# A 26-product scheme of 256-unit blocks in five of the seven outer terms of a graph network's adjacency products

## The chip, the cores and the metric

The kernel runs on one core of one Trainium2 chip. The metric is the device time of one execution in microseconds; the median of a few runs counts. The engines of the core are PE (matrix products; PEld is its weight load), DVE, ACT and POOL (elementwise work) and SP, which here only issues transfers. Each engine works through its own queue in order.

## The reference

Four layers on x, 8 batches x 2048 nodes x 64 features, with one 2048 x 2048 adjacency matrix A, all in float32. Each layer ends with `x = layernorm(x + layer(x))`.

```python
# layer 0: a weight matrix of its own for each node
w = einsum('nd,dkio->nkio', embedding, weight);  b = einsum('nd,do->no', embedding, bias)
As = [eye, A, 2 * (A @ A) - eye]
out0 = einsum('bnki,nkio->bno', einsum('knm,bmc->bnkc', stack(As), x), w) + b
# layer 1: twice  z = relu((A z) w_i)
# layer 2: x w_self + (A x) w_neigh + bias
# layer 3: [x, A x, 2 A A x - x, the last two again] w + bias
```

With the products by A regrouped this takes seven products of A with a 2048 x 512 matrix (512 = batch x feature): 1 and 2 in layer 0, 3 and 4 in layer 1, 5 in layer 2, 6 and 7 in layer 3.

## The kernel before

**Products 2 to 7** are calls of `product`. It cuts A into 2 x 2 blocks of 1024 and the right side into 2 x 2 quarters of 1024 x 256, and forms seven outer terms instead of eight (A11, S1, A12, S2, S4, S3, A22, in this order; S1 to S4 are sums of blocks of A). The sums of the right side are the tiles `T` (t1 to t4, DVE). Each outer term calls `inner`, which does the same once more with blocks of 512 and quarters of 512 x 128: four sums `t` on DVE (L258), and seven products `mul`, each of four matmuls with 512 moving columns (L286). In products 5 and 7 (`onto_slot`) the output stands the other way round, and a `mul` is sixteen matmuls with 128 moving columns (L279). `inner` works with three PSUM banks (mma, mmb, mmc); DVE and ACT add the results into tiles `C` (u, v, c), lines L229, L304, L332. From there `feature` functions are queued in a `Pump`, which puts a step of them behind each `mul`.

The blocks of A and of its sums come from memory in chunks of 1 MB, `load(q, s)`, seven to a term, through a ring of four buffers (seven after `to_late`), issued by SP. The sums of blocks (`comb`) are made in product 1 by `prepare` on DVE, and stored from POOL's queue by `keep`; of the four raw blocks of S1 to S4 `put` stores three.

**Layer 0's per-node product** (`feature0`) follows product 2's terms: 64 tiles of 128 nodes x 2 batches, four to a job. For each tile PE makes y in two halves (L1154; PSUM tiles `y`, three buffers). DVE multiplies the first half by the embedding and sums it into xy (eight times L1164); ACT does the second half (eight times L1168) into `s`, which POOL adds up in three halvings (L1173) and adds to xy (L1175). `s` has two buffers. The inputs xT and tT of a job are fetched on SP's queue when the job before it begins. `pump.run(n)` lets whole jobs run between terms: four jobs behind S2, four behind S3, and the other eight, 32 tiles, in product 3 behind its term A11.

The order on each engine is made at build time by a scheduler that goes by readiness and its own cost estimates; `keep_in_program_order` pins single instructions. What stands in one engine's queue is executed in that order, whatever comes earlier at run time.

`to_late` (called by product 3 through `between`) closes the pools of layer 0 and opens `p_mm2`, `p_z` and `ring2`. Before, product 3 called it behind S1.

Of the kernel before, what the change touches and what calls it, by code (L numbers as in the profile page):

```python
# [16 lines left out]
P = 128  # L17
# [4 lines left out]

A11, A12, A22, S1, S2, S3, S4 = range(7)
A21 = 7

DONE = (0, 3, 2, 1)


class Pump:


    def __init__(self):
        self.jobs = []
        self.later = []
        self.rate = 1
        self.gate = None
        self.owed = 0
        self.hold = False  # L40

    def add(self, gen):
        self.jobs.append(gen)
# [28 lines left out]
                if next(job[2], "done") == "done":  # L72
                    self.later.remove(job)

    def run(self, n=None):

        while self.jobs and n != 0:
            for _ in self.jobs[0]:
                self.tick()
            self.jobs.pop(0)  # L80
            n = None if n is None else n - 1

    def step(self, n=1, now=False):
        if self.jobs and self.hold and not now:
# [20 lines left out]
def kernel(  # L105
# [26 lines left out]
    NP = B // 2  # L132
    DH = D // 2
    RING = 4
    BLK = TG * GW

    big = ctx.enter_context(tc.tile_pool(name="big", bufs=1))
# [11 lines left out]


    comb = [dram.tile([8, P, BLK], F32, tag=f"comb{q}", name=f"comb{q}") for q in range(7)]

    def slice_chunk(ns, j, parts=(TG,)):

# [41 lines left out]
    banks = 0  # L196
    p_mm2 = None

    def load(q, s):
        nonlocal loads  # L200
        loads += 1
        turn = loads % (RING + 3)
        pool = ring2 if ring2 is not None and turn >= RING else ring
        a = pool.tile([P, TG, TG, P], F32, tag="a", name="a")
        if q in (A11, A12, A22) and s < 4:
            i, j = {A11: (0, 0), A12: (0, 2), A22: (2, 2)}[q]
            fetched = nc.sync.dma_start(a, blocks[i + s // 2, j + s % 2])
        else:
            fetched = nc.sync.dma_start(a, comb[q][s].rearrange("p (n m c) -> p n m c", n=TG, m=TG))
        if ring2 is not None and loads <= RING + 3:  # L210

            tc.keep_in_program_order(fetched)
        if pieces and loads > RING and loads % 3 == 0:
            tc.keep_in_program_order(pieces.pop(0)())
        return a

    def product(src, feature, between=None, rate=1, own=None, pin=False, runs=None, onto_slot=None, ends=False):

# [14 lines left out]
        def new_c():  # L235
            return sums.tile([P, 4, GW], F32, tag="C", name="C", bufs=4)

        def inner(q, b, finish, early=None, tail=None, next_sum=None, home=None):


# [7 lines left out]
            def new():  # L248
                if places:
                    return places.pop(0)  # L250
                return sums.tile([P, TG, 2 * F], F32, tag="t", name="t", bufs=5)


            pin = tc.keep_in_program_order if places else lambda inst: inst
# [13 lines left out]
            def mul(ps, s, xb, start, stop=True):  # L268
# [19 lines left out]
                        stop=(m == TG - 1), skip_group_check=True,  # L288
                    )
                pump.step(pump.rate)  # L290

            def bank(n):
                nonlocal banks
                banks += 1
                pool = p_mm if p_mm2 is None or banks % 3 else p_mm2
                return pool.tile([P, GW], F32, tag="mm", name=f"mm{n}")

            pa, pb = bank("a"), bank("b")
            mul(pa, 0, b11, True)
# [29 lines left out]
        def fresh(c):  # L329
            def finish(blk, ps, plus):  # L330
                if plus is None:
                    nc.scalar.copy(c[:, blk, :], ps)  # L332
                else:
                    add(c[:, blk, :], ps, plus)
            return finish,

        def onto(c, base, give=None, then=None):

            def early(blk, plus):
                add(c[:, blk, :], base[:, blk, :], plus)  # L340
                if give is not None and onto_slot is not None:
                    add(tiled(c[:, blk, :]), place(*give, blk), tiled(c[:, blk, :]))

            def finish(blk, ps, plus):
                if give is not None and onto_slot is not None:
                    if plus is None:
                        add(place(*give, blk), place(*give, blk), tiled(base[:, blk, :]))
                    add(place(*give, blk), tiled(ps), place(*give, blk) if plus is None else tiled(c[:, blk, :]))
                else:
                    add(c[:, blk, :], ps, (base if plus is None else c)[:, blk, :])  # L350
                if give is not None:
                    hand_over(c, *give, blk)
                if then is not None:
                    then(blk)
            return finish, early
# [56 lines left out]
        def prior(ih, ch):  # L412
# [5 lines left out]


        pump.pass_mark()  # L420
        u, v = new_c(), new_c()

        home = new_c() if runs is not None else None
        t1 = new_t()
        inner(A11, b11, *fresh(u), home=home, next_sum=lambda: tc.keep_in_program_order(
            nc.vector.tensor_tensor(t1, b12, b11, ALU.subtract)
        ))
        if pump.hold:
            pump.run()
            pump.hold = False  # L430
        inner(S1, t1, *fresh(v))
        pump.drain()
        pump.rate, pump.hold = rate, runs is not None
        runs = runs or {}
        if between is not None:
            between()
        t2 = new_t()
        sub = nc.vector.tensor_tensor(t2, b22, t1, ALU.subtract)
        if pin:
            tc.keep_in_program_order(sub)  # L440
        prior(0, 0)
        c = new_c()
        inner(A12, b21, *onto(c, u, (0, 0)))
        pump.run(runs.get(A12, 0))
        t3 = new_t()
        sub = nc.vector.tensor_tensor(t3, b22, b12, ALU.subtract)
        if pin:
# [2 lines left out]
        prior(0, 1)  # L450
        prior(1, 0)
        c = new_c()
        inner(S2, t2, *onto(u, u, then=lambda blk: add(c[:, blk], u[:, blk], v[:, blk])))
        pump.run(runs.get(S2, 0))
        inner(S4, b22, *onto(c, c, (0, 1)))
        pump.run(runs.get(S4, 0))
        pump.mark()
        prior(1, 1)

# [3 lines left out]
                add(place(1, 1, blk), place(1, 1, blk), tiled(v[:, blk]))  # L463
            hand_over(v, 1, 1, blk)

        inner(S3, t3, *onto(u, u, then=last))
        pump.run(runs.get(S3, 0))
        inner(A22, t4, *onto(u, u, (1, 0)), tail=at_the_end(u, 1, 0) if ends else None)

    def to_nodes(dst, pool, tiles, p, hT):  # L470

# [8 lines left out]
    class Norm:  # L480
# [23 lines left out]
        def square(self, pool=False, t0=0, t1=TG):  # L504
            if t0 == 0:
                if self.n == 1:
                    self.sq = sums.tile([P, TG, 2, F], F32, tag="t", name="sq1", bufs=5)
                else:
                    self.sq = small.tile([P, TG, 4, F], F32, tag="sq", name="sq")
            if pool:  # L510

                nc.gpsimd.tensor_tensor(self.sq, self.v, self.v, ALU.mult)
            else:
                self.pin(nc.scalar.activation(self.sq[:, t0:t1], self.v[:, t0:t1], AF.Square))
# [79 lines left out]
    if True:  # L594
# [7 lines left out]

        def load_weights():
            nc.gpsimd.memset(wd, 0.0)
            w3 = sums.tile([P, 5, F], F32, tag="t", name="w3", bufs=5)
            for k in range(2):
                half = slice(k * F, (k + 1) * F)
                for to, src in (
                    (wd[half, W1A, half], w_l1[0]), (wd[half, W1B, half], w_l1[1]),
                    (w2o[half, 0], w_neigh), (w2o[half, 1], w_self),  # L610
                ):
                    nc.sync.dma_start(to, src)
                nc.scalar.dma_start(w3[half], w_l3.rearrange("(k i) o -> i k o", i=F))
            nc.sync.dma_start(b2, b_l2.to_broadcast([P, F]))
            nc.sync.dma_start(b3, b_l3.to_broadcast([P, F]))
            return w3
# [24 lines left out]
        def prepare(ns, ch, outers):  # L641
# [41 lines left out]

            def put(q, s):
                flat = s.rearrange("p a b c -> p (a b) c")
                keep(q, 0, flat[:, :2])
                keep(q, 3, flat[:, 3:])
                inner(q, *(flat[:, k].rearrange("p (m n) -> p m n", m=TG) for k in range(4)))


# [37 lines left out]
        with tc.tile_pool(name="p_n", bufs=4, space=PSUM) as p_n, tc.tile_pool(  # L728
# [75 lines left out]
                    tc.keep_in_program_order(stored)  # L804

            def new_h():
                return sums.tile([P, GW], F32, tag="t", name="hT", bufs=5)

            def by_tiles(v):

# [276 lines left out]
        if True:  # L1087
# [89 lines left out]


            RUNS = {A12: 1, S2: NP, S3: NP}
            product(1, then(feature0, 0, gap=4, pool_sq=True), lambda: pump.add(sum_wn()), rate=4, runs=RUNS)  # L1180


    late = p_z = None

    def to_late():
        nonlocal late, p_z, p_mm2, ring2, loads
        first.close()
        late = ctx.enter_context(tc.tile_pool(name="late", bufs=1))
        ring2 = ctx.enter_context(tc.tile_pool(name="ring2", bufs=3))
        loads = 0  # L1190
        p_mm2 = ctx.enter_context(tc.tile_pool(name="p_mm2", bufs=1, space=PSUM))
        p_z = ctx.enter_context(tc.tile_pool(name="p_z", bufs=5, space=PSUM))

    def pair_transposed(g, p, slot):
        pt = p_z.tile([P, GW], F32, tag="z", name="pt2")
# [23 lines left out]
        nc.vector.scalar_tensor_tensor(part(g, p, 0), z, 0.0, part(g, p, 0), ALU.max, ALU.add)  # L1219
        yield  # L1220

    product(0, feature1a, to_late, pin=True)
    def both_terms(src, w, b):

        def own(g, p):
# [24 lines left out]
        yield from ()  # L1250


    product(1, then(feature1b, 0, mean=True, after=both_terms(0, w2o, b2)), rate=2)
    product(0, then(nothing, 1), onto_slot=1)


    def feature3(g, p, hT):
        nc.vector.tensor_tensor(part(g, p, 0), project([(hT, W3AA)]), part(g, p, 0), ALU.add)
        yield

    product(1, feature3, own=both_terms(1, w3o, b3), rate=1.5)
    product(0, then(nothing, 1, single=[(1, 0)], store=True), rate=2, onto_slot=1, ends=True)
    pump.drain()


# [46 lines left out]
```

## Time and profile before

| what | value |
|---|---|
| median of 3 runs | 1663.77 us (1663.74 to 1663.97) |
| span of the profiled execution | 1662.2 us |
| PE busy | 1653.4 us, 99% |
| DVE busy | 965.3 us, 58% |
| ACT busy | 279.2 us, 17% |
| POOL busy | 245.5 us, 15%, none of it behind layer 0 |
| product 1 | 0 to 208 us |
| product 2 and per-node tiles | 208 to 732 us |
| products 3 to 7 (rest) | 732 to 1655 us |

The page gives one profiled execution: busy time of each engine, the span in 40 slices, the chain of work that ended last, groups of equal instructions (line, engine, what is written from what, shape, count | busy us, mean ns of one | idle time before them and what ended it), and DMA issues. A line number such as L286 is that of the kernel file before; the changed kernel has its own numbers. Matmuls overlap, so their durations are longer than the distance from one start to the next.

### The profile page before, as it was taken

The page shows a single profiled execution, that of the slowest core. Times are in us where ns is not written, and L with a number is a line of the kernel's source. Part 1 is how long each engine was busy: PE and PEld are TensorE (multiplying, and loading weights), DVE is VectorE, ACT ScalarE, POOL GpSimd, SP SyncE. Part 2 cuts the span into 40 slices and gives each one's busy share as a digit, 9 for nine tenths or more (in the row PEclk, how much of TensorE's full clock was granted, in tenths as well). Part 3 has the DMA queues.
Part 4 walks back from the last instruction along what each step waited for, and adds up shares of the span by engine and source line. Part 5 has one row for each costly group of instructions (what it writes and reads, how often), then busy time and mean ns, then how long its engine had stood idle before and what let it go on. Part 6 is the DMA issues. An engine that isn't in the chain of part 4 may idle for free.

```text
span 1662.2 us, 21348 instructions
## 1 busy us (share of the span) xinstructions
PE 1653.4 (99%) x8438; PEld 1059.7 (64%) x8438; DVE 965.3 (58%) x1735; ACT 279.2 (17%) x824; POOL 245.5 (15%) x333
## 2 busy tenths in 40 slices
PE   9999999999999999999999999999999999999998
PEld 6998844444444444444454455599997455579998
DVE  5996795656555456654434365873568344453657
ACT  0210100242142144430010011220001011100001
POOL 1221200253154156550000000000000000000000
PEclk9999999999999999999999999999999999999999
DMA  8998899505504600029877877657888866678984
GB/s 310 334 384 337 322 324 325 183 26 177 191 28 144 233 26 26 26 78 362 295 258 279 306 259 259 229 207 277 295 291 303 301 217 233 229 260 299 313 315 160
DMA packets 81283, 391.59 MB, mean 236 GB/s; under 512 B 9088, under 2 KB 25856, under 8 KB 41248
## 3 DMA queue, kind: packets, MB, share of 16 engines
q1 hardware_dynamic: 68288, 346.78, 59.2%
q0 software_dynamic: 11248, 42.08, 6.7%
q10 hardware_dynamic: 1648, 1.38, 0.3%
q8 instruction: 67, 1.10, 0.3%
q14 instruction: 32, 0.26, 0.0%
HBM read 339.87 MB, written 50.33 MB: 235 GB/s over the span
## 4 chain that ended last, share of the span: by engine, by line
PE 95%; DVE 3%; DMA 1%; issue 0%; SPq 0%; ACTq 0%; DVEq 0%
PE y L1154 20%; PE mmb L286 17%; PE mma L286 12%; PE mmc L286 12%; PE mmb L279 9%; PE mma L279 6%; PE ps_n L935 6%; PE mmc L279 6%; PE z L1206 3%; PE z L1235 2%; PE ps_i L849 2%; DMA xy<-in_x 1%; PE pt L1197 1%; DVE si L647 1%; PE ps_e L935 0%; DVE so L647 0%
## 5 line engine op out<-in xcount | busy, mean ns | idle before, releaser
L286 PE MATMUL mmb<-a,t 128*128 128x512 f32 x648 | 292.0, 593 | 0.0
L1164 DVE SCALAR_TENSOR_TENSOR xy<-y,e_sb,xy 128x128 f32<-128x128 f32 x512 | 179.6, 351 | 141.2 <-PE y L1154 125.3
L286 PEld LDWEIGHTS mmb<-a,t 128*128 128x128 f32 x648 | 121.5, 190 | 145.3 <-issue 143.5
L1173 POOL TENSOR_TENSOR s<-s 128x512 f32<-128x512 f32 (+2 forms) x192 | 157.1, 818 | 332.5 <-ACT s L1168 322.3
L1168 ACT ACTIVATE s<-y,e_sb 128x128 f32<-128x128 f32 x512 | 138.9, 382 | 232.2 <-PE y L1154 228.9
L229 DVE TENSOR_TENSOR u<-mmb,p 128x512 f32<-128x512 f32 x84 | 57.8, 688 | 175.0 <-PE mmb L286 119.6
L279 PE MATMUL mmb<-t,a 128*128 128x128 f32 x1344 | 156.9, 275 | 0.0
L279 PEld LDWEIGHTS mmb<-t,a 128*128 128x128 f32 x1344 | 153.4, 192 | 0.0
L1154 PE MATMUL y<-wn,xT 64*128 64x512 f32 x512 | 131.5, 590 | 0.0
L1154 PE MATMUL y<-wn,C 64*128 64x512 f32 x512 | 131.2, 589 | 0.0
L1154 PE MATMUL y<-wn,tT 64*128 64x512 f32 x512 | 131.2, 589 | 0.0
L286 PE MATMUL mma<-a,T 128*128 128x512 f32 x256 | 115.5, 594 | 0.0
L286 PE MATMUL mmc<-a,t 128*128 128x512 f32 x216 | 97.3, 592 | 0.0
L304 ACT COPY p<-mma 128x512 f32<-128x512 f32 x42 | 24.6, 586 | 408.6 <-PE mma L286 267.1
L1154 PEld LDWEIGHTS y<-wn,xT 64*128 64x128 f32 x512 | 49.3, 187 | 61.2 <-issue 60.7
L1154 PEld LDWEIGHTS y<-wn,C 64*128 64x128 f32 x512 | 49.6, 187 | 60.2 <-issue 60.2
L1154 PEld LDWEIGHTS y<-wn,tT 64*128 64x128 f32 x512 | 49.6, 187 | 60.3 <-issue 60.3
L286 PE MATMUL mma<-a,xy 128*128 128x512 f32 x192 | 86.5, 593 | 0.0
L286 PEld LDWEIGHTS mma<-a,T 128*128 128x128 f32 x256 | 47.6, 190 | 56.8 <-issue 56.5
L229 DVE TENSOR_TENSOR C<-mmc,C 128x512 f32<-128x512 f32 x48 | 33.2, 692 | 85.9 <-PE mmc L286 75.1
L286 PEld LDWEIGHTS mmc<-a,t 128*128 128x128 f32 x216 | 40.0, 190 | 45.4 <-issue 45.2
L286 PEld LDWEIGHTS mma<-a,xy 128*128 128x128 f32 x192 | 36.1, 190 | 44.0 <-issue 43.8
(174 smaller groups left out, 2129.7 us busy)
## 6 DMA issues: line engine op xcount, KB each, us to landing
a<-comb SPq DMA_DIRECT2D x240, 1024.0 KB, 4.9
a<-in_blocks SPq DMA_DIRECT2D x54, 1024.0 KB, 4.9
comb<-si POOLq DMA_DIRECT2D x28, 1024.0 KB, 8.4
a<-in_slices SPq DMA_DIRECT2D x15, 1024.0 KB, 10.5
comb<-so POOLq DMA_DIRECT2D x15, 512.0 KB, 8.9
t1T<-hT SPq DMA_DIRECT2D x16, 256.0 KB, 6.4
xT<-in_xT SPq DMA_DIRECT2D x16, 256.0 KB, 3.4
tT<-t1T SPq DMA_DIRECT2D x16, 256.0 KB, 3.3
```

The source lines that it names most:

```text
L229: nc.vector.tensor_tensor(out, a, b, op)
L279: nc.tensor.matmul(to, a[:, k, m, :], xb[:, m, :], start=(start and opens and m == 0), stop=(m == TG - 1), skip_group_check=True,)
L286: nc.tensor.matmul(ps, xb[:, m, :], a[:, :, m, :], start=(start and m == 0), stop=(m == TG - 1), skip_group_check=True,)
L304: nc.scalar.copy(p1, pa)
L849: nc.tensor.matmul(ps, x[:, m // 2, m % 2], s[n](m), start=(start and m == 0), stop=(m == TG - 1), skip_group_check=True,)
L935: nc.tensor.matmul(ps[:, ts(p, GW // 2)], b(k, p), a(k // TG, k % TG), start=(start and p == k == 0), stop=(k == NT // 2 - 1), skip_group_ ...
L1154: mm = nc.tensor.matmul(y[:, b, :], terms[n][half, ts(k, P)], wn[half, n, h * DH : (h + 1) * DH, :], start=(n == 0), stop=(n == 2),)
L1164: nc.vector.scalar_tensor_tensor(acc, y[:, :, ts(d, F)], e, acc, ALU.mult, ALU.add)
L1168: nc.scalar.activation(s[:, d], y[:, :, ts(d, F)], AF.Copy, scale=e)
L1173: nc.gpsimd.tensor_tensor(s[:, :n], s[:, :n], s[:, n : 2 * n], ALU.add)
L1206: nc.tensor.matmul(z[:, k, :], aT[:, ts(k, P)], wd[:, w, :], start=(n == 0), stop=(n == len(terms) - 1),)
L1235: nc.tensor.matmul(z[n][:, k], xT[half, ts(k, P)], w[half], start=True, stop=True)
```

## The change

For the five terms A11, S1, A12, S2 and S4 of products 3 to 7 (`FORMED`; not for S3 and A22) `inner` is replaced by `fast_inner`: A's 1024-block is cut 4 x 4 and the right side's 1024 x 256 quarter 4 x 2, and 26 products of 256-unit blocks take the place of seven products of 512-unit blocks. The 26 forms of the adjacency block no longer depend on the right side, and are made once: `make_forms(q)` loads four raw chunks, makes 28 sums of 512 elements a partition (22 on DVE, 6 on POOL) and stores 26 forms of 256 KB to memory from SP's queue, beside the per-node jobs. A11's are made behind S2, those of S1 and A12 behind S3, those of S2 and S4 before product 3's A11, which now stands behind the per-node jobs, as does `to_late`. The right side's forms (f1 to f6, d, fn, fm: seven sums of 512 elements and four of 256; `less` and `plus` call POOL) are made for each term; the results are joined on DVE and ACT.

Besides, the late part has four PSUM banks for products and four for `z` (three and five before), the tag `t` has nine buffers in place of five, `put` stores all four raw blocks in one transfer, and the scratch space for DMA descriptors is set to 8192.

```diff
+FORMED = (A11, S1, A12, S2, S4)
+PAIRS = (
+    (10, 24), (23, 14), (5, 16), (9, 25), (7, 3), (15, 18), (0, 21),
+    (13, 22), (8, 17), (2, 6), (20, 4), (11, 19), (1, 12),
+)
+POOLED = {25, 13, 17, 8, 22, 5}
...
-    def run(self, n=None):
+    def run(self, n=None, side=(), rate=1):
+        side, owed = list(side), 0
         while self.jobs and n != 0:
             for _ in self.jobs[0]:
                 self.tick()
+                owed += rate
+                while owed >= 1:
+                    owed -= 1
+                    if side and next(side[0], "done") == "done":
+                        side.pop(0)
...
+    def make_forms(q):
+        tiles = [load(q, s) for s in range(4)]
+        yield
...
+        for n, ik in RAW.items():
+            store(n, raw(*ik))
+        for n, a, b, sign in SUMS:
+            f = sums.tile([P, 2, 2, P], F32, tag="t", name="form", bufs=TB)
+            if sign == 0:
+                nc.vector.scalar_tensor_tensor(f, source(a), -1.0, source(b), ALU.mult, ALU.subtract)
+            else:
+                eng = nc.gpsimd if n in POOLED else nc.vector
+                eng.tensor_tensor(f, source(a), source(b), ALU.add if sign > 0 else ALU.subtract)
...
+                store(n, f)
+            yield
...
+        def fast_inner(q, b, to, begin=None, end=None):
...
+            f4, f3, f5, f6 = xt("f4"), xt("f3"), xt("f5"), xt("f6")
+            less(f4, two(xb(1, 0)), xp(2, 0))
+            less(f3, two(xb(0, 1)), xp(2, 1))
+            plus(f5[:, 0], f3[:, 0], f4[:, 1])
+            plus(f5[:, 1], f3[:, 1], f4[:, 0])
...
+            def mul(ps, n, h, start):
+                k = SLOT[n]
+                if k // 4 not in chunk:
+                    chunk[k // 4] = load(q, k // 4, True).rearrange("p f (n m) c -> p f n m c", n=2)
...
+                    for m in range(2):
+                        nc.tensor.matmul(
+                            ps[:, ts(h, GW // 2)], x[:, m, :], a[:, :, m, :],
+                            start=(start and h == m == 0), stop=(m == 1), skip_group_check=True,
+                        )
...
+            b1 = fill(bank("1"), True, PAIRS[0])
+            nc.scalar.copy(even, halves(b1))
+            b2 = fill(bank("2"), True, PAIRS[1])
+            nc.vector.tensor_tensor(odd[:, 1], even[:, 0], even[:, 1], ALU.add)
+            nc.scalar.copy(odd[:, 0], b2[:, : GW // 2])
+            nc.vector.tensor_tensor(odd[:, 0], odd[:, 0], b2[:, GW // 2 :], ALU.add)
+            b5 = fill(bank("5"), True, PAIRS[2])
+            rows(1, odd)
+            onto(c[2, 1], c[0, 0], halves(b5))
+            fill(b2, False, PAIRS[3])
+            join(even, b2, ALU.subtract)
...
-                keep(q, 0, flat[:, :2])
-                keep(q, 3, flat[:, 3:])
+                keep(q, 0, flat)
...
+        pace = 1.2
+        waits = pump.hold and A11 in fast
+        if waits:
+            pump.run(None, side(A11), pace)
+            pump.hold = False
+            begins()
...
-        pump.run(runs.get(S2, 0))
+        pump.run(runs.get(S2, 0), side(S2), pace)
...
-        pump.run(runs.get(S3, 0))
+        pump.run(runs.get(S3, 0), side(S3), 2 * pace)
...
-            product(1, then(feature0, 0, gap=4, pool_sq=True), lambda: pump.add(sum_wn()), rate=4, runs=RUNS)
+            product(1, then(feature0, 0, gap=4, pool_sq=True), lambda: pump.add(sum_wn()), rate=4, runs=RUNS, forms={S2: (A11,), S3: (S1, A12)})
...
-        p_mm2 = ctx.enter_context(tc.tile_pool(name="p_mm2", bufs=1, space=PSUM))
-        p_z = ctx.enter_context(tc.tile_pool(name="p_z", bufs=5, space=PSUM))
+        p_mm2 = ctx.enter_context(tc.tile_pool(name="p_mm2", bufs=2, space=PSUM))
+        p_z = ctx.enter_context(tc.tile_pool(name="p_z", bufs=4, space=PSUM))
...
-    product(0, feature1a, to_late, pin=True)
+    product(0, feature1a, to_late, pin=True, fast=FORMED, forms={A11: (S2, S4)})
...
+    nc = bacc.Bacc("TRN2", target_bir_lowering=False, num_devices=1, dynamic_dma_scratch_size=8192)
```

## The prediction

> **What bounds the kernel now.** I read the page's busy shares and chain first.
>
> ```profile
> PE 1653.4 (99%) x8438; PEld 1059.7 (64%) x8438; DVE 965.3 (58%) x1735; ACT 279.2 (17%) x824; POOL 245.5 (15%) x333
> PE 95%; DVE 3%; DMA 1%; issue 0%; SPq 0%; ACTq 0%; DVEq 0%
> ```
>
> PE is busy all the time and carries the chain, so matmul time removed is time gained, unless PE then waits for something. What a matmul costs is read from start to start in the timeline of PE, since its durations overlap.
>
> ```profile
> 412.40 3.60 PE L286 MATMUL mma<-a,T 128*128 128x512 f32 x8
> 415.83 3.60 PE L286 MATMUL mmb<-a,t 128*128 128x512 f32 x8
> ...
> 436.53 1.13 PE L1154 MATMUL y<-wn,xT 64*128 64x512 f32 x4
> ...
> 171.39 3.62 PE L935 MATMUL ps_n<-a,xy 128*128 128x256 f32 x16
> 174.85 0.60 PE L474 MATMUL pt_n<-ident,hT 128*128 128x128 f32 x4
> ...
> 1483.68 3.57 PE mmb L279 x32
> 1494.40 3.57 PE mmc L279 x32
> ```
>
> Each program matmul leaves two records. Eight records of 512 columns take 3.43 us, so an outer term of seven products (56 records) takes 24.03 us. Sixteen of 256 columns take 3.46 us, 0.216 each. The last two lines (chain of waits) are three products apart: 32 records of 128 columns take 3.573 us, 0.1117 each, and a term of the onto_slot kind 25.01 us.
>
> Then two stretches by window: S2's inner term and the per-node work behind it.
>
> ```profile
> 281.29:305.32 24.03, 24.03 (x57) 10.46 (x56) 18.77 (x24) 0.58 (x1) 0.00 (x0) 1.00 0.91 332
> 305.32:388.01 82.69, 82.69 (x385) 37.10 (x384) 45.51 (x128) 33.86 (x121) 44.75 (x60) 1.00 0.14 44
> ```
>
> Columns: length, then busy us of PE, weight load, DVE, ACT and POOL, clock, DMA share, GB/s. The second holds 16 per-node tiles, 82.69 / 16 = 5.15 us each on PE (24 records), and DVE is idle for 45% of it, which is where the change puts its sums. Last, the groups that price DVE and POOL, and one collision of the two in the timelines of DVE and POOL:
>
> ```profile
> L1164 DVE SCALAR_TENSOR_TENSOR xy<-y,e_sb,xy 128x128 f32<-128x128 f32 x512 | 179.6, 351 | 141.2 <-PE y L1154 125.3
> L258 DVE TENSOR_TENSOR t<-T,t 128x512 f32<-128x512 f32 x48 | 32.9, 685 | 0.0
> L1173 POOL TENSOR_TENSOR s<-s 128x512 f32<-128x512 f32 x64 | 81.0, 1266 | 322.5 <-ACT s L1168 322.3
> L1173 POOL TENSOR_TENSOR s<-s 128x256 f32<-128x256 f32 x64 | 47.0, 735 | 5.0
> ...
> 393.30 1.38 DVE L229 TENSOR_TENSOR C<-C,p 128x512 f32<-128x512 f32 x1 [0.68 <-ACT p L304]
> 396.81 2.38 DVE L229 TENSOR_TENSOR C<-C,u 128x512 f32<-128x512 f32 x1
> ...
> 392.87 2.93 POOL L1173 TENSOR_TENSOR s<-s 128x512 f32<-128x512 f32 x3 [4.17 <-ACT s L1168]
> 396.41 2.22 POOL L512 TENSOR_TENSOR sq<-xy 128x1024 f32<-128x1024 f32 x1
> ```
>
> The two DVE sums cost 0.69 us elsewhere and took 1.38 and 2.38 us here: both operands lie in SBUF and POOL was inside a sum of its own. L1164, with y from PSUM, stays at 351 ns under POOL.
>
> **Part 1, the gain on PE.** A fast term has 26 products of two 256-column matmuls: 104 records x 0.216 = 22.46 us, against 24.03: 1.57 saved. There are 15 of these (five terms of products 3, 4 and 6): 23.5 us. The onto_slot kind has 208 records x 0.1117 = 23.23 against 25.01: 1.78 saved, in ten terms: 17.8 us. Sum 41.3 us, all on the path as long as PE stays fed. The weight loads double in number in the first kind; the 256-column rows already load weights for each matmul and hold 0.216, so that costs nothing.
>
> **Part 2, making the adjacency forms.** Five times `make_forms`: 22 sums on DVE, 6 on POOL, 26 stores of 256 KB and 4 loads of 1 MB on SP's queue. As totals they fit: 110 DVE sums x 0.69 = 76 us, against an idle 5.15 - 8 x 0.351 = 2.34 us in each of 64 tiles, 150 us. But the built order of the changed kernel doesn't spread them. DVE runs its queue in order. With Y for an L1164 of a tile, F a form sum and t an L258-like sum, it reads:
> - behind S2 (tiles 1 to 3): 8Y; 10F, 8Y with 7F between; 5F, 8Y with 7t between; then Y alone for 13 tiles
> - behind S3 (17 to 22): 8Y with 7F; 6F, 8Y with 7F; 2F, 8Y; 8Y; 9F, 8Y with 7F; 5F, 8Y with 1F and 4t
> - before product 3 (33 to 38): the same 44F, without the t.
>
> So 22 sums fall on about 2.5 tiles, nearly 9 to a tile where 2.34 / 0.69 = 3.4 fit. What is late next is PE: y has three buffers, a tile uses two, so the second half of tile k+1 waits until DVE has drained the first half of tile k. Over k tiles DVE needs k x 2.81 + n x 0.69, PE k x 5.15, so PE loses 0.69 n - 2.34 k: 29 x 0.69 - 3 x 2.34 = 13.0; 48 x 0.69 - 6 x 2.34 = 19.1; 44 x 0.69 - 6 x 2.34 = 16.3. Together 48.4 us. It isn't made up later, as PE is the bound in the tiles that follow.
>
> **Part 3, DVE against POOL.** Of these 121 sums all have both operands in SBUF. POOL is busy for 44.75 / 82.69 = 54% of such a stretch. Hit in half of the cases, for some 0.45 us (what is left on average of a POOL sum of 0.45 to 1.27): 121 x 0.54 x 0.45 = 29 us; I take 29. Bounds: 0 if DVE's sums fall into POOL's pauses, 121 x 0.69 = 83 if each is hit as the 1.38 row was.
>
> [...]
>
> **Part 4, the loads of the second set.** SP is in order too: behind S3 the four loads of the second set, and the xT of the next job, stand behind the last store of the first set. 4.2 MB at the 332 GB/s of the window row take 12.6 us; the Y of two tiles (5.6 us) covers part, and 7 us remain, at two places (S3 and product 3): 14 us. Bounds 0 and 25.
>
> **Part 5, the late products.** A fast term's input sums are moved to POOL: seven of 1.27 and four of 0.735 are 11.8 us in 22.46, and POOL does nothing else there. DVE rises from 6.2 to 9.1 us a term (nine to thirteen L229 and L258 rows) to 11.7 (eleven sums of 512 elements, two of 1024 at 1.22, four of 256 at 0.42). Both are covered on average. The couplings are shorter: the fourth pair of products accumulates into the bank of the second, and in between ACT and DVE (0.37 + 0.42 us) must have read it, in 1.73 us: 0.9 us of slack, where one product of 3.43 us left 2.7 before. In a few terms the built order puts a 2.28 us sum (T2, T3) or a normalization just there. I put this at 10 us, bounds 0 and 40 (25 terms x 1.6). The clears on POOL and the copies on ACT lie beside matmuls. In front, `put` stores all four blocks: 16 x 256 KB more, in slices of the page with a DMA share of 8 or 9 tenths; nothing waits there for a load today: 0, at most 12 us. Product 3's A11 moves behind the per-node work: no row is added by that, though its ring2 loads now wait for the last tiles; it is inside the 10.
>
> **The sum**, against the profiled span of 1662.2: -41.3 + 48.4 + 29 + 14 + 10 = +60, a span of 1722. The median of the runs is 1663.77, 1.6 above the span; the same distance gives 1724.
>
> A stall could cost once more. The `rise` matmuls, the program's first, have a mean of 427 ns at L738, where L849's of the same shape have 275, so PE starts slow; in the rest the granted clock is 1.00. [...]
>
> **Rivals.**
> - *The sums hide after all* (faster). The totals speak for it: 76 us in 150 us of idle DVE. It decides if no more than 3.4 sums fall to a tile, or if the y buffers carry the lag. Then only part 1 and some of part 5 remain: 1663.8 - 41.3 + 0 to 10 = 1622 to 1633. Against it: the built order, with 16 and 17 sums before single tiles. Chance 0.12.
> - *The bursts alone*: POOL pauses when DVE sums, loads come in time. 1663.8 - 41.3 + 48.4 = 1671, to 1690 with part of the rest. Chance 0.18, of which 0.03 lies within 0.2% of the time before.
> - *The late products stall too*: the 0.9 us of slack is missed in most of 25 terms, at 2 us each 50 in place of 10: 1764, and with more collisions up to 1800. [...] Against it: DVE and POOL are near 52% of a term. Chance 0.17.
> - *The forecast*: 1690 to 1755, chance 0.53.
>
> **How the numbers follow.** 1724 is the forecast's sum. The range of 1672 to 1768 leaves out the faster rival and some 0.07 above. A measurement of this kernel can tell about 0.2% (3.3 us) from no change: faster 0.12, same 0.03, slower 0.85.
>
> **What would show it** (with lines of the changed kernel: L1505 is Y, L290 F). Right: PE's waits name y behind L1505, PE's idle time lies in the first tiles behind S2 and S3 and before product 3 (some 20, 35 and 35 us), the form sums (L290) have a mean well over 0.69, and a fast term of product 5 or 6 takes near 22.5 (23.2) us plus its features. Wrong: if PE is busy without a gap in the per-node stretches; if L290 stays at 0.69 (then part 3 falls); if the idle time lies in the late products (then the third rival); or if 256-column matmuls take more than 0.216.

## The result, and the profile after

The changed kernel takes 1799.1 us (median of 4 runs, 1797.9 to 1800.8), the kernel before 1663.8: a ratio of 1.081, 95% interval 1.080 to 1.083. The forecast was 1724 with a range of 1672 to 1768: the sign was right, the size was far too small. The spans are 1799.0 and 1662.2 us, so there are 136.8 us to account for. Times of single runs below have no interval.

Busy shares, granted clock in 40 slices and the chain's engines, from the page of the changed kernel:

```profile
PE 1653.8 (92%) x8998; PEld 1199.5 (67%) x8998; DVE 1198.3 (67%) x1967; ACT 302.1 (17%) x867; POOL 664.2 (37%) x640
PEclk9999999799879986999899999999999999999999
PE 49%; DVE 10%; POOL 1%; ACT 1%; issue 1%; DVEq 0%; ACTq 0%; POOLq 0%
```

PE had 99% of its span and now has 92%; the chain, 95% PE before, goes through DVE for 10%; and the clock row, which was all nines, has six slices under 9. All of them lie in the first half of the span. The waits of PE (line, releaser: us in total, times, longest):

```profile
PE y L1495 <- DVE xy L1505: 112.4, 12, 18.1
PE mm L435 <- DVE u L477: 6.8, 3, 4.3
PE mm L435 <- ACT s L1509: 4.6, 1, 4.6
PE mm L435 <- DVE p L468: 2.7, 1, 2.7
```

Ten of the 12 waits of y behind L1505, 102.0 us, are the stall that was forecast. The stretch behind S2, by window, against the row of before that the prediction shows:

```profile
305.44:388.00 82.56, 61.79 (x269) 28.46 (x270) 59.31 (x120) 22.10 (x82) 43.42 (x46) 0.88 0.50 171
```

PE is busy for 61.79 of 82.56 us where it was busy throughout, DVE for 59.3 where it was 45.5, and the mean clock is 0.88. Inside it, PE's timeline (start, length, idle time before it):

```profile
319.52 1.02 PE L1495 MATMUL y<-wn,tT 64*128 64x512 f32 x4
320.38 1.02 PE L1495 MATMUL y<-wn,C 64*128 64x512 f32 x4
333.18 2.08 PE L1495 MATMUL y<-wn,xT 64*128 64x512 f32 x4 [11.77 <-DVE xy L1505]
335.05 1.92 PE L1495 MATMUL y<-wn,tT 64*128 64x512 f32 x4
336.75 1.09 PE L1495 MATMUL y<-wn,C 64*128 64x512 f32 x4
346.84 2.08 PE L1495 MATMUL y<-wn,xT 64*128 64x512 f32 x4 [9.00 <-DVE xy L1505]
```

Groups of four records start 0.86 us apart at the top. Behind the stall of 11.77 us they start 1.87 and 1.70 apart: PE runs at half speed for its first 3.6 us, and after one group at full speed it stalls again. The window of these 3.7 us has a clock of 0.50 (the third number from the end):

```profile
332.90:336.60 3.70, 3.42 (x8) 1.52 (x10) 3.67 (x5) 0.00 (x0) 3.33 (x3) 0.50 0.72 267
```

That second cost is what the forecast's sum left out. What DVE and POOL did in the meantime, and the groups of DVE's sums (busy us, mean ns | idle before, releasers):

```profile
320.24 1.64 DVE L290 TENSOR_TENSOR form<-a,form 128x512 f32<-128x512 f32 x1
321.80 1.21 DVE L290 TENSOR_TENSOR form<-a 128x512 f32<-128x512 f32 x1
...
325.77 1.71 DVE L290 TENSOR_TENSOR form<-form,a 128x512 f32<-128x512 f32 x1
327.40 0.34 DVE L1505 SCALAR_TENSOR_TENSOR xy<-y,e_sb,xy 128x128 f32<-128x128 f32 x1
327.67 1.48 DVE L290 TENSOR_TENSOR form<-a 128x512 f32<-128x512 f32 x1
```

```profile
319.62 1.71 POOL L290 TENSOR_TENSOR form<-form 128x512 f32<-128x512 f32 x1
321.29 2.03 POOL L1514 TENSOR_TENSOR s<-s 128x256 f32<-128x256 f32 x2
...
325.67 1.27 POOL L290 TENSOR_TENSOR form<-form 128x512 f32<-128x512 f32 x1 [1.49 <-DVE form L290]
326.89 3.70 POOL L1514 TENSOR_TENSOR s<-s 128x512 f32<-128x512 f32 x3
```

```profile
L290 DVE TENSOR_TENSOR form<-a 128x512 f32<-128x512 f32 x45 | 49.4, 1103 | 28.7 <-DMA a<-comb 17.2 <-DMA a<-in_blocks 11.4
L1505 DVE SCALAR_TENSOR_TENSOR xy<-y,e_sb,xy 128x128 f32<-128x128 f32 x512 | 178.3, 349 | 121.7 <-PE y L1495 108.4
```

DVE's sums of 0.69 us take 1.2 to 1.7 while POOL is in a sum of its own, and L1505, with y from PSUM, keeps a mean of 349 ns under the same POOL work. All 110 form sums on DVE took 117.8 us, a mean of 1.07.

The other two waits of y, of 5.24 us each, lie in tiles far behind the form sums, in which layer 0's result is normalized:

```profile
728.94 3.06 DVE L1505 SCALAR_TENSOR_TENSOR xy<-y,e_sb,xy 128x128 f32<-128x128 f32 x8 [2.10 <-PE y L1495]
738.99 1.22 DVE L863 TENSOR_REDUCE ss<-sq 128x16 f32<-128x1024 f32 x1 [7.00 <-POOL sq L854]
```

```profile
744.44 2.08 PE L1495 MATMUL y<-wn,xT 64*128 64x512 f32 x4 [5.24 <-DVE xy L1505]
```

Here DVE does nothing for 7.00 us: the normalization's sum `ss` stands in its queue ahead of the next tile's L1505 and waits for POOL's squares `sq`, which stand behind POOL's halvings of s. PE runs out of y buffers meanwhile.

A fast term of product 4 runs as forecast, 20 records in 4.32 us, 0.216 each:

```profile
1081.85 1.89 PE L435 MATMUL mm<-a,fn 128*128 128x256 f32 x8
1083.58 1.03 PE L435 MATMUL mm<-a,fm 128*128 128x256 f32 x4
1084.44 1.89 PE L435 MATMUL mm<-a,f 128*128 128x256 f32 x8
1086.17 3.62 PE L435 MATMUL mm<-a,xy 128*128 128x256 f32 x16
```

**The account.** The rows come from PE's timeline: start-to-start distances without the idle times, the idle times, and in the stretches of half clock half of the time in which PE worked.

| part | forecast | measured |
|---|---|---|
| matmuls of products 3 to 7 | -41.3 | -37.2 |
| PE idle in the per-node stretches | 48.4 + 29 + 14 = 91.4 | 20.8 + 40.9 + 40.3 = 102.0 |
| PE idle in two tiles with a normalization | 0 | 10.5 |
| PE idle in the late products | 10 | 24.2 |
| work at half clock, 15 stretches | 0 | 33.2 |
| y and z matmuls a little further apart | 0 | 4.1 |
| sum | +60 | +136.8 |

### The profile page after: what moved, and what is told of

The parts are those of the page before. It is cut to its first block, busy times and chain, and to the rows that moved or that the text cites. A ratio compares the mean times of both kernels' runs of the same rounds, so it can differ in the third digit from the quotient of the medians.

```text
span 1799.0 us, 23675 instructions
## 1 busy us (share of the span) xinstructions
PE 1653.8 (92%) x8998; PEld 1199.5 (67%) x8998; DVE 1198.3 (67%) x1967; ACT 302.1 (17%) x867; POOL 664.2 (37%) x640
## 4 chain that ended last, share of the span: by engine, by line
PE 49%; DVE 10%; POOL 1%; ACT 1%; issue 1%; DVEq 0%; ACTq 0%; POOLq 0%
PE mm L435 16%; PE mm L429 11%; PE y L1495 7%; PE mmb L554 3%; PE mmb L547 2%; PE mmc L554 2%; PE z L1547 2%; PE mma L554 2%; PE mma L547 2%; PE mmc L547 1%; PE z L1576 1%; DVE C L310 1%; DVE ss L863 1%; DVE xy L884 1%; DVE C L458 1%
## 5 line engine op out<-in xcount | busy, mean ns | idle before, releaser
L1505 DVE SCALAR_TENSOR_TENSOR xy<-y,e_sb,xy 128x128 f32<-128x128 f32 x512 | 178.3, 349 | 121.7 <-PE y L1495 108.4
L1495 PE MATMUL y<-wn,xT 64*128 64x512 f32 x512 | 145.5, 642 | 112.4 <-DVE xy L1505 112.4
L1514 POOL TENSOR_TENSOR s<-s 128x512 f32<-128x512 f32 (+2 forms) x192 | 170.5, 888 | 136.0 <-ACT s L1509 126.3
L435 PE MATMUL mm<-a,f 128*128 128x256 f32 x720 | 174.1, 388 | 14.0 <-DVE u L477 6.8
L435 PEld LDWEIGHTS mm<-a,f 128*128 128x128 f32 x720 | 138.7, 195 | 36.2 <-DVE u L477 8.7
L554 PE MATMUL mmb<-a,t 128*128 128x512 f32 x288 | 129.5, 592 | 0.0
L429 PE MATMUL mm<-f,a 128*128 128x128 f32 x960 | 115.8, 275 | 2.4 <-DVE u L477 2.4
L429 PEld LDWEIGHTS mm<-f,a 128*128 128x128 f32 x960 | 111.3, 192 | 2.9 <-DVE u L477 2.7
L468 DVE TENSOR_TENSOR p<-p,mm 128x512 f32<-128x512 f32 x75 | 51.3, 684 | 72.0 <-PE mm L435 52.1
L458 DVE TENSOR_TENSOR C<-C,mm 128x512 f32<-128x512 f32 x105 | 71.3, 684 | 41.0 <-PE mm L435 30.7
L381 POOL TENSOR_TENSOR f<-xy 128x512 f32<-128x512 f32 x30 | 40.9, 1378 | 153.7 <-PE mm L435 96.1
L554 PEld LDWEIGHTS mmb<-a,t 128*128 128x128 f32 x288 | 53.7, 190 | 62.7 <-issue 62.4
L554 PE MATMUL mma<-a,T 128*128 128x512 f32 x160 | 72.2, 594 | 0.0
L435 PE MATMUL mm<-a,xy 128*128 128x256 f32 x288 | 69.3, 383 | 0.1
```

Of the source, the lines that this page charges most:

```text
L381: nc.gpsimd.tensor_tensor(out, a, c, ALU.subtract)
L429: nc.tensor.matmul(ps[:, ts(2 * h + j, P)], a[:, j, m, :], x[:, m, :], start=(start and h == j == m == 0), stop=(m == 1), skip_group_check ...
L435: nc.tensor.matmul(ps[:, ts(h, GW // 2)], x[:, m, :], a[:, :, m, :], start=(start and h == m == 0), stop=(m == 1), skip_group_check=True,)
L458: nc.vector.tensor_tensor(out, out, view(v), op)
L468: nc.vector.tensor_tensor(e, e, halves(ps), op)
L554: nc.tensor.matmul(ps, xb[:, m, :], a[:, :, m, :], start=(start and m == 0), stop=(m == TG - 1), skip_group_check=True,)
```

## The experiments

An overview first. The time is the median (one execution for e1, e3, e4, e5 and e9); the other columns are of the profiled execution, and "half clock" is the number of stretches and the time lost in them:

| run | time us | y waits of PE | all idle of PE | half clock |
|---|---|---|---|---|
| the change | 1799.1 | 112.4 | 137.4 | 15, 33.2 |
| e1_pinned | 1727.2 | 50.4 | 76.8 | 9, 17.8 |
| e2_even | 1711.3 | 36.2 | 68.4 | 5, 10.0 |
| e3_forms_only | 1815.2 | 114.5 | 122.3 | 13, 25.8 |
| e4_no_sums | 1671.2 | 8.7 | 33.1 | 5, 10.9 |
| e5_no_s_sums | 1765.8 | 82.8 | 104.2 | 15, 32.2 |
| e6_fill | 1795.1 | 47.2 | 70.3 | 11, 21.2 |
| e7_a11_old | 1792.2 | 109.9 | 129.6 | 15, 29.6 |
| e8_four_sets | 1703.2 | 9.9 | 47.8 | 7, 14.3 |
| e9_no_pool | 1745.3 | 68.3 | 87.7 | 13, 26.3 |
| e10_late_close | 1786.1 | 110.3 | 124.4 | 14, 30.1 |
| e11_best | 1682.1 | 25.8 | 35.1 | 6, 14.3 |
| e12_three_sets | 1681.2 | 7.8 | 27.2 | 2, 3.4 |
| e13_four_apart | 1680.6 | 10.7 | 33.1 | 4, 6.7 |

**Is it the place of the sums?** First each form sum pinned to its place in the program, then the sets spread as well.

```diff
-                eng.tensor_tensor(f, source(a), source(b), ALU.add if sign > 0 else ALU.subtract)
+                made = eng.tensor_tensor(f, source(a), source(b), ALU.add if sign > 0 else ALU.subtract)
+            tc.keep_in_program_order(made)
```

> The change with each form sum pinned behind what was recorded before it on its engine, rates as they are: DVE's queue then holds 1 to 3 sums ahead of a tile behind S2 and before product 3, and 3 to 5 behind S3. Theory (the bursts in DVE's order starve PE, and the gaps halve PE's clock): the 112 us that PE waited for y fall to 5 to 25 us, all behind S3 (44 sums x 1.07 less 12 tiles x 2.34 of slack = 19), and most of the 36 us at half clock go with the long gaps: 1665 to 1690 us. Rival (the collisions of DVE and POOL in SBUF are the cost, in whatever order the sums stand): the sums keep a mean of 1.07 us, and some 40 us of waiting stay: 1715 to 1740 us. Rival (the cost lies in products 3 to 7): no change, 1790 us or more.

Measured 1727.2, in the range of the second theory. The pin alone gives back 72 us: y waits fall from 112.4 to 50.4 us in shorter pieces (19, at most 10.7), and the half clock with them. But DVE's form sums still take 0.83 to 1.10 us by group (0.95 in the mean), and their waits for blocks stay at 26.8 us. In the second run one set lies behind S2, one behind S3 and three before product 3:

```diff
-        pace = 1.2
+        pace = 1.0
-            pump.run(None, side(A11), pace)
+            pump.run(None, side(A11), 1.4)
-        pump.run(runs.get(S3, 0), side(S3), 2 * pace)
+        pump.run(runs.get(S3, 0), side(S3), pace)
-... forms={S2: (A11,), S3: (S1, A12)})
+... forms={S2: (A11,), S3: (S1,)})
-... forms={A11: (S2, S4)})
+... forms={A11: (A12, S2, S4)})
```

> As the pinned version, with the sums spread evenly: one set behind S2, one behind S3 (rate 1.0), three before product 3 (rate 1.4), so 1 to 3 sums ahead of each tile everywhere. Theory: PE hardly waits for y (under 8 us); left are the 41 us of gain, some 26 us of waits in products 3 to 7 and up to 10 us at half clock: 1650 to 1662 us, faster than both kernels. Rival (collisions): 1700 us or more. Rival (cost in products 3 to 7): 1790 us.

Measured 1711.3, ratio 1.029 (1.027 to 1.031): 88 us better than the change and still slower than before: the expectation failed, and the time lies in the range of the rival that puts the cost down to the collisions. Its waits, from its own list:

```profile
PE y L1496 <- DVE xy L1506: 36.2, 13, 8.3
PE mm L436 <- DVE ss L864: 14.0, 1, 14.0
```

The 14 us are new: the last set's sums end with the last per-node tile, and the normalization behind them makes product 3's A11 late (DVE's ss there waits 6.5 us for POOL's squares, as in the two tiles above).

**Which half of the change costs?** First the forms made as in the change, products 3 to 7 on the old scheme (`fast=()`); then the reverse, the fast scheme with no form summed.

> The forms are made as in the change (same side jobs, same free scheduling), but products 3 to 7 use the old scheme, so that the forms are never read. Theory: all of the waiting for y stays (some 110 us) and some 30 us at half clock, and nothing is gained: 1795 to 1815 us. Rival (the cost lies in products 3 to 7): 1680 us or less.

Measured 1815.2, as expected, with the same 12 waits of y (114.5 us). So making the forms, with A11 and `to_late` in their new places, costs 151 us by itself, and the fast terms bring only 16 us in the change, not 37: some 17 us of idle time in the late part and 7 of half clock come with them.

```diff
-            f = sums.tile([P, 2, 2, P], F32, tag="t", name="form", bufs=TB)
-            ...
-                formed_by[n] = f
-                store(n, f)
+            if n != "h":
+                store(n, raw(n % 4, n // 4 % 4))
```

> The change without the 28 sums of each form set: raw blocks are stored in the place of the sums (so the forms hold other values), with all loads and stores. Theory: PE doesn't wait for y; products 3 to 7 gain 41 us and lose some 26 us in waits and 6 at half clock: 1648 to 1660 us; the loads and stores cost nothing. Rival (the transfers are the cost): over 1690 us.

Measured 1671.2, 11 us above the expectation's upper end, and 7 us slower than before (one execution). With sums that cost nothing, 33 us of idle time remain; the longest waits:

```profile
PE y L1486 <- DMA xT<-in_xT: 6.6, 1, 6.6
PE mm L426 <- DVE u L468: 6.1, 2, 4.8
PE mm L426 <- ACT s L1500: 4.6, 1, 4.6
```

The xT of a job waits behind the forms' stores on SP's queue; the two of 4.8 and 4.6 us are at product 3's A11.

**Is it POOL that stretches DVE's sums?** L1514, the three halvings of s, removed:

> The changed kernel without POOL's three halvings of s (L1514); ACT still writes s and POOL still adds its first slice to xy, so that DVE's and PE's work stays as it is and POOL's 2.9 us a per-node tile fall to 0.45. That part of the sum over the embedding is left out. If DVE's form sums are stretched by POOL's reads of SBUF, their mean falls from 1.07 us to 0.70 to 0.75, 110 sums give back some 35 us of stall, the waits of y fall from 112 to some 75 us, and the time is 1750 to 1765. If the stretch has another cause (the form sums meeting transfers, or only their place), the mean stays over 1.0 and the time over 1790. If the collisions were the whole loss, it would be under 1700.

Measured 1765.8. The mean of a form sum falls from 1.07 only to 0.90 us, so this is a part of it: 18.4 of the 42 us of stretch. What POOL still does there is mostly its own form sums:

> As the run without POOL's halvings of s (again left out), and the six form sums of each set that POOL made are made by DVE too, so that in the per-node stretches POOL only adds one 128-column slice a half tile. If the rest of the stretch of DVE's form sums (0.90 us a sum in that run, 0.69 in sums that meet no POOL work) comes from POOL's own form sums, the mean of L290 falls to 0.68 to 0.75, and the time stays within some 15 us of 1766, since DVE then makes 140 sums in place of 110. If it comes from transfers or from ACT, the mean stays at 0.85 or more and the time rises by some 25 us.

```profile
L290 DVE TENSOR_TENSOR form<-a 128x512 f32<-128x512 f32 x60 | 40.7, 683 | 32.0 <-DMA a<-in_blocks 14.7 <-DMA form<-a 11.0 <-DMA a<-comb 6.3
L290 DVE TENSOR_TENSOR form<-form 128x512 f32<-128x512 f32 x30 | 21.1, 703 | 0.4
```

The sums are back at 0.68 to 0.70 us, with the same loads and stores in flight: the stretch comes from POOL's work. The time, 1745.3, is better than expected: DVE does 30 sums more and the kernel is 20 us faster.

**Does a stall cost again in clock?** PE repeats the first half of y where it would stand still.

```diff
+            REPEAT = {3: 4, 4: 3, 22: 6, 23: 3, 38: 6, 39: 2, 46: 2, 50: 2}
...
-                        for n in range(3):
+                        again = REPEAT.get(4 * order.index((g, p)) + k + 1, 0) if h == 0 else 0
+                        for n in [*range(3)] * (1 + again):
```

> The changed kernel, in which PE repeats the first half of y (the same six matmuls into the same tile) in eight per-node tiles where it then stands still: 4, 3, 6, 3, 6, 2, 2 and 2 times, 2.57 us each, sized to stay under the idle times of 11.8, 9.0, 17.5, 8.2, 18.1, 5.5, 5.2 and 5.2 us. DVE's and POOL's work is the same, and nothing waits for the repeats. If the clock falls to half because PE stands still, and each stall of over some 4 us costs about 2.2 us more in work at half speed (the 8 stretches of half clock in question held 18.0 us of such loss), the clock stays at 1.00 in these places and the time falls by 15 to 20 us, to 1779 to 1784, though PE does 72 us more work. If the fall of the clock has another cause, or costs nothing, the time stays at 1799 or rises.

Measured 1795.1 (ratio to before 1.079, 1.077 to 1.080), with 72 us of additional matmuls and yet 4 us less. The same window in the change and in this run:

```profile
512.00:556.00 44.00, 18.34 (x66) 8.07 (x64) 35.40 (x58) 6.08 (x23) 24.62 (x22) 0.69 0.74 256
```

```profile
512.00:556.00 44.00, 39.64 (x178) 18.39 (x176) 36.56 (x58) 5.35 (x21) 24.67 (x22) 0.96 0.76 262
```

The clock goes from 0.69 to 0.96 although DVE and POOL do the same work. In the eight places the loss at half clock falls from 18.0 to 5.1 us; the rest follows idle times that were left (5.8, 2.2 and 2.3 us). The profiled execution is 8.0 us shorter than the change's, the median 4.0. That this is less than the 12.9 us has a reason: idle and filling together are 142.3 us against 137.4, 4.5 of it in one tile, where the scheduler put eight sums t ahead of the L1505 group instead of between. In the other seven places idle time, filling and half-clock loss together fall by 10.9 us, for 12.8 us less of half clock, so most of what is lost at half clock is lost in time. That the clock falls where PE stands still is shown; the expected size was not reached.

**The late waits.** Product 3's A11 on the old scheme (`fast=FORMED[1:]`, with the per-node work still ahead of it), and then `to_late` behind this term:

> The changed kernel with the old seven products of 512-unit blocks in product 3's A11 alone; its place, the forms and everything else stay. If the two idle times there (4.6 and 4.3 us, with half clock behind each, 5.3 us lost) come from the short distance between pairs of products and the elementwise work that must lie between them, they go, against 1.6 us more on PE: 1785 to 1789. If they come from what DVE and ACT still have to do for layer 0, whatever the scheme, the wait stays in the same term or moves to S1, and the time is 1797 to 1803.

Measured 1792.2 (1.077, 1.076 to 1.079), between the two theories, because there were two causes. The second idle time (4.3 us) went, the first stayed, now released for mma. It is the next run's question:

```diff
-            begins()
...
+        if waits:
+            begins()
```

> The changed kernel with the old products in product 3's A11, as in the run before, and to_late called behind this term instead of ahead of it. In that run the first product of A11 still stood idle for 4.55 us, released by ACT's last sum of a per-node tile. If that is the PSUM space of y, which to_late hands to the new banks while ACT still reads it, the wait goes, and the half clock behind it (1.7 us): 1784 to 1788 against 1792. If A11 waits for data that the last tile still has to write, the wait stays, and the time is 1790 to 1794.

Measured 1786.1 (1.074, 1.072 to 1.075), as the theory of the PSUM space has it. The run moves all pools that `to_late` opens, the SBUF pools too; that ACT released the wait, not a load, speaks for the PSUM space. PE's timeline in the change, and in this run:

```profile
849.10 1.03 PE L1495 MATMUL y<-wn,C 64*128 64x512 f32 x4
854.69 3.75 PE L435 MATMUL mm<-a,f 128*128 128x256 f32 x8 [4.56 <-ACT s L1509]
858.23 4.06 PE L435 MATMUL mm<-a,xy 128*128 128x256 f32 x16
866.58 6.76 PE L435 MATMUL mm<-a,f 128*128 128x256 f32 x16 [4.29 <-DVE u L477]
```

```profile
847.13 1.04 PE L1496 MATMUL y<-wn,C 64*128 64x512 f32 x4
848.10 3.70 PE L554 MATMUL mma<-a,xy 128*128 128x512 f32 x8
```

In the change the eight records behind the first idle time are 3.54 us long together and the sixteen behind the second 6.6, where full speed takes 1.73 and 3.46. With `to_late` behind it, A11 starts without a pause.

**Is there a version that gains?** Four attempts, all built from the evenly spread run with product 3's A11 on the old scheme and xT and tT fetched from ACT's queue. First four sets, with empty steps behind each set's loads:

```diff
-FORMED = (A11, S1, A12, S2, S4)
+FORMED = (A11, S1, A12, S2)
...
-        yield
+        for _ in range(6):
+            yield
```

> The evenly spread version, with four sets in place of five (S4 on the old scheme throughout: 8.3 us less gain), one behind S2, one behind S3, two before product 3; six empty steps behind the loads of each set, so that its sums come when the blocks have landed; product 3's A11 on the old scheme; xT and tT fetched from ACT's queue, not behind the forms' stores in SP's. If what was left of the loss is the head of line at each set's loads, the sums that end together with the last per-node tile, and the late A11, the time is 1650 to 1666: 1664 - 31 + some 12 of y waits + 12 of late stalls and clock. If each set costs some 8 us wherever its sums are put (POOL's and DVE's collisions in every tile), it is 1675 to 1690.

Measured 1703.2 (1.023, 1.022 to 1.025): missed. The y waits are down to 9.9 us, but the empty steps push the last sums to the end of each stretch, and the next outer term's loads stand behind the forms' stores on SP's queue: four waits of mma and mmb for blocks, 24 us together. Then shorter pauses, higher rates and `to_late` behind A11:

> Four sets (S4 on the old scheme), pinned at one to three sums a tile: rate 1.2 behind S2 and S3 with two empty steps behind the loads, 1.3 before product 3 with five, so that each stretch ends with several tiles free of form sums; product 3's A11 on the old scheme and to_late behind it; xT and tT from ACT's queue. On PE four terms in five give 28.5 us (37.2 measured for 25 terms; 19 terms remain). If the loss is only a matter of place, some 10 us of y waits, 6 of late waits and 6 of half clock remain: 1655 to 1667, no slower than before. If each form sum costs PE time wherever it stands, about 6 us a set as in the evenly spread run, it is 1672 to 1685.

Measured 1682.1 (1.011, 1.009 to 1.012), in the range of the theory against place. But the built order showed why: where form sums end, the eight sums t of the next term are drawn forward into one tile. Two more runs pin those and keep the sums away from the normalizations:

```diff
-            pin = tc.keep_in_program_order if places else lambda inst: inst
+            pin = tc.keep_in_program_order if places or runs or waits else lambda inst: inst
```

> Three sets (A11, S1, A12; S2 and S4 on the old scheme), one behind S2, one behind S3, one before product 3, each at two or three sums a tile and ended five or more tiles before the stretch ends and before the two normalizations; the old scheme's sums t (L526) pinned to their own place, since in the run before they were drawn into the tile behind the last form sum. A11 of product 3 and to_late as in that run. On PE 20.9 us of gain (9 terms of 512 columns at 1.40, less product 3's A11, 6 of 128 columns at 1.62, as measured). If a form sum costs PE time only where it meets another lump of DVE work (t, a normalization, a load), hardly any y wait is left, late waits and their half clock take some 9, and the time is 1652 to 1660, faster than before. If every form sum costs PE time wherever it stands (6 us a set), it is 1667 to 1675.

> The same with S2's set as a fourth, started 25 steps later so that its sums lie behind the two normalizations. 28.5 us of gain on PE. By the theory of place it is some 5 us faster than the run with three sets, 1648 to 1658, unless its sums, which end two tiles before product 3's A11, make that term late (then about equal to it). By the theory of a price for each sum it is 1666 to 1676.

Measured 1681.2 (1.011, 1.010 to 1.013) and 1680.6 (1.010, 1.008 to 1.011): above what both theories said. None of the four versions is faster than the kernel before. The waits of the run with three sets:

```profile
PE mmb L556 <- DVE t L528: 9.0, 3, 3.0
PE y L1499 <- DVE xy L1509: 7.8, 11, 0.9
PE mm L437 <- DVE p L470: 2.7, 1, 2.7
```

The clock is back at 0.997. The 20.1 us that three sets bring on PE are eaten by 26.5 us more idle time (9.0 for the pinned t, 7.8 for y, the rest in late products and pieces under 1 us), 3.4 of half clock and some 5.7 of matmuls further apart. The bursts are a matter of place: 11 waits of at most 0.9 us are left of 12 of up to 18.1, although a form sum on DVE takes 1.09 us here too (71.7 us for 66). A smaller price remains wherever the sums stand: y waits and y matmuls further apart are 11.5 us for 66 sums on DVE, 0.17 each, against 1.0 in the change.

## Why the prediction was wrong

**The step that failed is the clock.** The text says that a stall could cost once more, and its sum counts nothing for it. By the account it costs 33.2 us, the largest of the missing terms: with it alone the sum would have been 1757, inside the range. In the profile of the change all 14 idle times of PE from 4.29 to 18.08 us end in a stretch at clock 0.50. Each stretch is a multiple of 3.41 us long (3.41 to 20.5), and all of them begin on one grid of 3.41 us. A shorter idle time than such a step can be enough: 2.19 us (from 1190.13) was followed by a stretch of 3.41 us, 2.66 us (from 1431.43) and everything under 2.19 by none. In the run with the filled stalls two idle times of 2.18 us went either way: behind the one that ends at 533.14 the groups of y start 1.87 and 1.61 us apart, behind the one that ends at 547.54 0.93 and 0.86. A stall costs 2.2 us more in work at half speed (33.2 / 15), and there were 12 in the per-node stretches and three later. That the rows of before showed only clock 1.00 was no reason to count nothing: they held no stall (no wait of PE over 1.1 us in that profile). The filled stalls show the cause; they got back 8 us of a profiled execution, 4 of the median, so that 33.2 is the account's figure and not one that a run gave back in full.

**Part 1, the gain:** 37.2 instead of 41.3. The medians of 0.216 and 0.112 us a record hold; over whole terms the means are 0.218 and 0.1127. What makes the few longer distances was not looked into.

**Part 2, the bursts:** right in place and mechanism. The waits of y are behind L1505, in the forecast places: 20.8, 40.9 and 40.3 us against "some 20, 35 and 35 us". (A slip in the sum: 82.69 / 16 is 5.17, not 5.15, which would take 0.3 us off the 48.4.) Reading the built order of DVE, not the totals, gave this.

**Part 3, the collisions:** right in kind, as the run without POOL's sums shows (0.68 to 0.70 us a form sum there, 1.07 in the change); the size was 42 us of longer sums in place of 29. The term counted POOL at the 54% of before and forgot that six sums of each set go to POOL itself, into the same bursts.

**A part that was missing altogether:** the two tiles with a normalization, 10.5 us of idle time and 4.7 of half clock. This is no collision: DVE stands idle for POOL's squares, 7.00 us each time. Without POOL's halvings that wait is 2.60 us and PE's 2.37, and in the run with no form summed, where DVE's queue has the next tile's L1505 ahead of `ss`, PE doesn't wait there.

**Part 4, the loads:** DVE's form sums waited for blocks for 28.7 us, twice the 14. With this and the measured sums in the forecast's formula, parts 2 to 4 give 48.4 + 42 + 28.7 = 119; the three places lost 102.0, so some 17 us of DVE's delay did not reach PE.

**Part 5, the late products:** 24 us in place of 10. Of this, 4.6 us are a wait that the text passed over: with `to_late` ahead of A11, the new banks take y's PSUM space while ACT still reads the last tile. That "no row is added by that" was wrong. 4.3 us are the coupling that was named: the sum that reads the second bank (L477) stood on DVE behind layer 0's last normalization, which waited 5.4 us for POOL's squares (L854), and behind a T sum of 2.28 us. The rest are pieces of 0.1 to 2.7 us.

**The rivals:** the hidden sums are excluded by the run with the forms only, and the bursts alone (1671 to 1690) by the form sums of 1.07 us and the 28.7 us that they waited for blocks. The third rival's range reaches up to 1800 and takes in the measured time, but not by its mechanism: the late products lost 24 us, not 50. What the forecast named is there; its time, 1690 to 1755, was missed by what it left out or made too small. The missing 76.7 us are 33.2 (clock), 14.2 (late), 10.6 (the three places), 10.5 (normalizations), 4.1 (gain) and 4.1 (y and z).

## What to carry to other kernels

Count the stalls of a change as well as their length: in the kernel before PE had no wait over 1.1 us and a clock of 0.999, and in the change 15 pauses of 2.19 to 18.08 us cost 33.2 us at half clock on top of 137.4 us of standing still. Where one engine's queue is ordered at build time, read that order before comparing totals, and look too for an instruction that waits for another engine ahead of work that is ready: with 110 sums in bursts PE waited 102 us for y behind them, with 66 at two or three a tile 7.8. And an algorithm that saves 6% of the matmul time of the terms that it changes (37.2 of some 610 us) has only that to spend; here even the run with no form summed was 7 us slower than before, with waits for xT, for PSUM banks and for the sums that read them.

## What was not expected of the hardware

Filling a stall with useless matmuls made the kernel no slower: with 72 us of repeats in place of idle time the clock in one window rose from 0.69 to 0.96, and the time fell by 4 us (0.2%). And moving 30 sums from POOL to the busier DVE made it 20 us faster (1765.8 to 1745.3, both without the halvings), with DVE's sums back from 0.90 to 0.69 us.
